# A graph layer on one core: a weight slice loaded ahead of the edge line, transposes behind three products, and a new order for gathers and sums

## The chip, the core and the metric

The kernel runs on one core of a Trainium2 chip. The core has a matrix engine (TensorE, called PE in the profile, with its weight loads as PEld), a vector engine (VectorE, DVE), an activation engine (ScalarE, ACT), a general engine (GpSimd, POOL) and a queue engine for transfers (SyncE, SP). Each engine works through its own list of instructions strictly in order and waits on semaphores for the others. The metric is the device time of one execution in microseconds, as the median of several executions. The kernel before takes 260.74 us as the median of three (260.15, 260.74 and 263.15 us).

## The reference

A layer of a relational graph network on 625 nodes of width 512 and 20,625 edges, sorted by destination, followed by a feed-forward net. Cut to what matters:

```python
h   = relu(layernorm(x))                                  # 625 x 512
msg = sum over r of (h[src] @ W_rel[r] + b_rel[r]) * where(edge_type == r, edge_weight, 0)
agg = segment_sum(msg, dst) / max(segment_sum(edge_weight, dst), 1)
x1  = layernorm(h + h @ W_self + b_self + agg, ln1)
ffn = gelu(x1 @ W_ffn1 + b_ffn1) @ W_ffn2 + b_ffn2        # 512 -> 1024 -> 512
out = x + layernorm(x1 + ffn, ln2)
```

## The kernel before

The nodes lie in five blocks of 128 rows (block 1 has 113). The **first part** makes a table of 20 x 128 rows, the product of every block with each of the four relation weights, scaled and with the bias added. For each of the 20 steps `table_rows` (L391) puts four products into one accumulation bank; one 128x512 product in plain fp32 is two PE instructions in the profile (L403). VectorE scales the result (L416) and SP stores it to the table in memory. During the first relation the transposed form of the next block is made between the products: `between()` turns it with four transposes (L351) into a bank, and ScalarE copies it out (L357) for the next step. The loads at the program's start stand in one list on SP (L262 to L278): halves of x, four slices of the first relation's weight, the line of edges that the first address arithmetic reads, further blocks of x, and so on. SP works through them in that order. In the same part GpSimd scatters 45 columns of edge weights into a memory area of cells (L686), from which the sums of the first and last block are later made as dense products (L1302, L613).

The **second part** handles the blocks in between by gathers. GpSimd issues 99 indirect transfers of 128 table rows each (L1159) and six smaller-purpose ones of the same size (L1216, the first edges of a block that begin in a foreign group). They go into ten buffers called `ms`. Three gathers make one group: ScalarE scales the first row into a PSUM bank called `add` (L1165), VectorE adds the second and the third (L1183), and PE multiplies the sum with a one-hot matrix and accumulates it by destination node. This last product comes in two forms. A **whole** sum is written to SBUF by the third addition (`es`) and multiplied in plain fp32 (L1208). A **parted** sum stays in the bank; ScalarE casts a high part (`eh`, L1169), VectorE subtracts it to get a low part (`el`, L1173), and PE multiplies both in the fp32r format (L1205, L1206). The groups are worked by blocks: single tiles of the outer boundaries first, then block 1, the boundary of 1 and 2, block 2, the boundary of 2 and 3, and block 3 with nine groups and one single tile at the end. When a block's sums are complete VectorE normalises it, PE transposes it (L351), ScalarE copies it (`x1T`, L1363), PE makes the 1024 hidden values in eight pieces (L928), ScalarE applies the gelu to each piece (L932) and PE makes the 512 outputs (L946). The feed-forward nets follow in the block order 0, 4, 1, 2, 3.

The order of everything in the second part on every engine is laid out when the program is built. The class `Plan` walks through time with an estimate for each operation and lets each engine take the operation of best rank among those that are ready; the resulting lists are then fixed. For a gather it assumes a landing `LAND` after its issue, and for the earliest gathers `LATE` more: pairs of a gather number and the addition for gathers below it. Which groups are parted is decided by `parted` from the pair `PARTED` (of the second number of consecutive groups the first number are parted). Idle PE time in the last block's tail is filled with small dummy products (`spin`, L1226).

Of the kernel before, what the change touches and what calls it, by code (L numbers as in the profile page):

```python
# [154 lines left out]
def gnn_layer(ctx, tc, x, edges, edge_line, edge_groups, w_self, w_rel, w_ffn1, w_ffn2, rows_in, bf1_in, out, n_edges):  # L155
# [19 lines left out]
    KD = D // P  # L175
# [52 lines left out]
    def load_x(b0, b1):  # L228
        nc.sync.dma_start(xs[:, b0:b1, :], x[ep.first[b0]:ep.first[b0] + (b1 - b0) * P, :].rearrange("(b p) d -> p b d", p=P))

    def load_wr(r, ks=((0, KD),)):
        wr_sb.setdefault(r, None)
        if wr_sb[r] is None:
            wr_sb[r] = early.tile([P, KD, D], F32, tag="wr", name=f"wr_{r}", bufs=2)
        for k0, k1 in ks:
            nc.sync.dma_start(wr_sb[r][:, k0:k1, :],
                              w_rel[r, :, k0:k1, :])
# [27 lines left out]
    load_wr(0, [(1, 2)])  # L265
    load_x(1, 2)
    load_wr(0, [(2, 3)])
    load_line(0)
    load_wr(0, [(3, 4)])
    load_x(2, 3)  # L270
    load_rows(brel_bc[:, :D], 0, D)
    load_x(3, NB)
# [121 lines left out]
    def table_rows(r, i, between=None):  # L394
        c = r * NB + i
        cuts = (0, 3 * D // 4, D) if c == NC - 1 else (0, D)
        at = [slice(*h) for h in zip(cuts, cuts[1:])]
        p = [buffer("ps") for h in at]
        for p_, h in zip(p, at):
            for k in range(KD):  # L400
                if k == KD // 2 and between:
                    between()
                nc.tensor.matmul(p_[:, :h.stop - h.start], hT[i][:, k, :], wr_sb[r][:, k, h],  # L403
                                 start=(k == 0), stop=(k == KD - 1))
        if c >= NL:
            m = kept[c] = const.tile([P, D], F32, name=f"m_{c}")
        else:
            k = (c + NL) % CH
            if k == 0 or c == 0:
                kept["pair"] = const.tile([P, CH, D], F32, tag="tr", name=f"tr_{c}", bufs=LA)  # L410
            m = kept["pair"][:, k, :]
            if c in held:
                kept[OUTER[0], c] = m
        row0 = r * NP + i * P
        for p_, h in zip(p, at):
            made_row.append(nc.vector.scalar_tensor_tensor(m[:, h], p_[:, :h.stop - h.start], rx[:, i, 1:2],  # L416
                                           brel_bc[:, r * D + h.start:r * D + h.stop], op0=ALU.mult, op1=ALU.add).ins)
            stored.append(nc.sync.dma_start(table[row0:row0 + P, h], m[:, h]).ins)
# [589 lines left out]
    SUM = 3  # L1008
    WARM = 24
    ES = 7  # L1010
    LAND, LATE = 3.6, ((8, 2.0), (40, 1.2))
    HOTS_AT, SELF_AT, ADDS_AT = (15, 16, 17), 15, (16, 17, 18)
    OHS = 3
    OW = 5
# [1 line left out]
    GATHER = 1.26  # L1016
    SLACK = 1.2
    LATER = 0.3
    PARTED = 1, 1
    BEHIND = 5  # L1020
    CELLS = 3.0
    FIRST_PIECE = 4
# [102 lines left out]
    order_of = sorted(of_sum, key=lambda bs: (not set(bs) & set(OUTER), -bs[0] if set(bs) & set(OUTER) else bs))  # L1125
# [37 lines left out]
    def first_row(j, ms, box):  # L1163
        box["sum"] = buffer("add")
        nc.scalar.activation(box["sum"], ms[j], AF.Copy, scale=wgt[:, j:j + 1])  # L1165
# [6 lines left out]
        box["low"] = edge.tile([P, D], F32R, tag="es", name=f"el_{j}", bufs=ES)  # L1172
        nc.vector.tensor_sub(box["low"], box["sum"], box["high"].bitcast(F32))  # L1173

    def parted(k, units):
        return len(units[k]) > 1 and k % PARTED[1] < PARTED[0] and k + 3 < len(units)

    def row_added(j, ms, box, parts):
        k, q = divmod(j - GROUP0, EG)
# [51 lines left out]
    for bs in order_of:  # L1231
        tiles = of_sum[bs]
        units = []
# [13 lines left out]
        for k, unit in enumerate(units):  # L1247
# [15 lines left out]
            for q, (j, g) in enumerate(zip(unit, got)):  # L1263
                alone, whole = len(unit) == 1, q == len(unit) - 1
                if alone:
                    h = g
                elif q == 0:
                    h = row0 = op("ACT", 0.69, lambda j=j, box=box: first_row(j, ms, box), after=[g],
                                  take=["add"], give=[("ms", g)], lag=SLACK, rank=rank)
                else:  # L1270
                    parts = parted(k, units)
                    h = op("DVE", 0.75, lambda j=j, box=box, parts=parts: row_added(j, ms, box, parts), after=[g, h],
                           take=["es"] if whole and not parts else [],
                           give=[("ms", g)] + ([("add", row0)] if whole and not parts else []), lag=LATER, rank=rank)
                    h_last = h
                    if whole and parts:
                        h = op("ACT", 0.65, lambda j=j, box=box: high(j, box), after=[h], take=["es"], rank=rank)
                        h = op("DVE", 0.7, lambda j=j, box=box: low(j, box), after=[h], take=["es"], give=[("add", row0)], lag=0.6, rank=rank, level=0.7)
            end = unit is units[-1]
            parts = parted(k, units)  # L1280
            m = op("PE", 0.47 if parts else 0.87,
                   lambda bs=bs, k=k, q=k - k0, end=end, ohs=ohs, box=box, j=unit[0]: edge_sum(bs, k, q, end, ohs, box, j),
                   after=[h, hots_op, m], take=["acc"] if k == 0 else [],
# [290 lines left out]
```

## Time and profile before

| quantity | value |
|---|---|
| median of the timed executions | 260.74 us |
| the profiled execution | 262.26 us |
| its span from the first to the last instruction | 260.5 us |
| PE busy | 246.4 us, 95% |
| VectorE busy | 200.5 us, 77% |
| GpSimd busy | 172.0 us, 66% |
| ScalarE busy | 74.8 us, 29% |

A row of the timeline gives the start in us, the duration in us (of several merged instructions if it ends in x4, x16 and so on), the engine, the line, the operation and its tiles; a bracket holds the idle time of the engine just before it and what ended that. A row of the chain gives start, duration, engine, tile and line. A row of a table by stretches gives the stretch, its length, and for PE, PEld, DVE, ACT and POOL the busy time and the number of instructions, then the granted PE clock, the share of the transfer engines and GB/s.

### The profile page before, as it was taken

Reading aid. Unit: us, or ns where it says so; the run is one execution under the profiler, and the core shown is the slowest. Engines: PE = TensorE matmul, PEld = TensorE weight load, DVE = VectorE, ACT = ScalarE, POOL = GpSimd, SP = SyncE. Lnnn points to the kernel's source line nnn. Section 1 sums busy time; section 2 is a strip of 40 time slices with the busy share of each in tenths; the row PEclk is TensorE's granted clock in tenths of the full one; section 3 lists DMA queues with packets and bytes.
Section 4 is the critical chain, followed back from the end, with each engine's and each line's share of the span. In section 5 each row is a group of like instructions: output and inputs, shape, how many; then the busy total and the mean of one; then the engine's idle time right before and its main releaser. Section 6 shows DMA issues by size and latency. Waiting matters only on the chain. (4 is left out here: it accounts for less than half of the span.)

```text
span 260.5 us, 3515 instructions
## 1 busy us (share of the span) xinstructions
PE 246.4 (95%) x1051; PEld 141.4 (54%) x1051; DVE 200.5 (77%) x503; ACT 74.8 (29%) x224; POOL 172.0 (66%) x230
## 2 busy tenths in 40 slices
PE   8899999999999969999959999989999998899996
PEld 6444444445445625443424444864685964675964
DVE  2896999997979964839879399997798985973614
ACT  3017300000031573623121142641223632310420
POOL 4478889887888577777778777777777777100000
PEclk9999999999999999999999999999999999799999
DMA  5999999972272599799997977777776677330101
GB/s 191 361 402 416 379 382 360 321 285 81 73 253 85 199 363 328 227 346 299 367 325 219 374 232 201 218 191 208 213 212 205 199 204 213 111 110 6 44 0 44
DMA packets 24055, 60.20 MB, mean 231 GB/s; under 512 B 4401, under 2 KB 8753, under 8 KB 22882
## 3 DMA queue, kind: packets, MB, share of 16 engines
q0 software_dynamic: 9936, 27.58, 35.0%
q1 hardware_dynamic: 13808, 30.94, 32.1%
q10 hardware_dynamic: 290, 1.44, 1.6%
q8 instruction: 9, 0.15, 0.2%
q14 instruction: 12, 0.10, 0.1%
HBM read 50.77 MB, written 9.17 MB: 230 GB/s over the span
## 5 line engine op out<-in xcount | busy, mean ns | idle before, releaser
L1159 POOL DMA_INDIRECT ms<-table,row_i x99 | 97.2, 982 | 30.8 <-issue 13.4
L403 PE MATMUL ps<-wr,hT 128*128 128x512 f32 (+2 forms) x168 | 71.2, 576 | 0.0
L686 POOL DMA_INDIRECT cells<-weight,cell x45 | 48.6, 1080 | 9.0 <-issue 6.4
L403 PEld LDWEIGHTS ps<-wr,hT 128*128 128x128 f32 x168 | 30.6, 190 | 33.8 <-issue 29.9
L1183 DVE SCALAR_TENSOR_TENSOR add<-ms,wgt_g,add 128x512 f32<-128x512 f32 x48 | 35.7, 748 | 16.8 <-DMA ms<-table,row_i 14.9
L928 PEld LDWEIGHTS ps<-x1T,w_sb 128*128 128x128 f32 x320 | 39.1, 197 | 5.2 <-issue 3.2
L928 PE MATMUL ps<-x1T,w_sb 128*128 128x128 f32 (+1 forms) x320 | 39.7, 281 | 0.9 <-ACT gT L932 0.9
L1165 ACT ACTIVATE add<-ms,ed 128x512 f32<-128x512 f32 x30 | 20.7, 692 | 66.5 <-DMA ms<-table,row_i 47.3
L946 PE MATMUL ps<-w_sb,gT 128*128 128x512 f32 (+3 forms) x96 | 36.2, 522 | 0.0
L1302 PE MATMUL acc<-tr,sums_w 128*128 128x512 f32 x60 | 27.7, 595 | 0.0
L599 ACT ACTIVATE ohw<-os,w 128x128 fp32r<-128x128 f32 x36 | 11.4, 389 | 56.3 <-DVE os L581 55.3
L946 PEld LDWEIGHTS ps<-w_sb,gT 128*128 128x128 f32 (+1 forms) x96 | 16.6, 188 | 14.4 <-issue 11.8
L932 ACT ACTIVATE gT<-ps,bf 128x128 f32<-128x128 f32 (+1 forms) x40 | 13.3, 362 | 19.6 <-PE ps L928 14.9
L441 PE MATMUL ps<-ws_sb,hT 128*128 128x512 f32 x40 | 18.3, 592 | 0.0
L1302 PEld LDWEIGHTS acc<-tr,sums_w 128*128 128x128 f32 x60 | 11.0, 190 | 12.3 <-issue 11.2
L1208 PE MATMUL acc<-es,oh 128*128 128x512 f32 x24 | 12.9, 626 | 3.2 <-DVE es L1183 3.2
L416 DVE SCALAR_TENSOR_TENSOR tr<-ps,rx,brel_bc 128x512 f32<-128x512 f32 x15 | 11.2, 744 | 3.3 <-POOL idle L689 2.1
L1173 DVE TENSOR_TENSOR el<-add,eh 128x512 fp32r<-128x512 f32 x18 | 12.3, 681 | 0.9 <-ACT eh L1169 0.8
L1169 ACT CAST eh<-add 128x512 fp32r<-128x512 f32 x18 | 10.5, 581 | 8.2 <-DVE add L1183 8.2
L956 DVE TENSOR_TENSOR ow<-ps,z 128x512 f32<-128x512 f32 (+3 forms) x6 | 3.6, 599 | 11.4 <-PE ps L946 11.3
L441 PEld LDWEIGHTS ps<-ws_sb,hT 128*128 128x128 f32 x40 | 7.6, 190 | 8.7 <-issue 8.6
L1205 PE MATMUL acc<-eh,oh 128*128 128x512 f32 x18 | 11.7, 651 | 0.0
(215 smaller groups left out, 302.5 us busy)
## 6 DMA issues: line engine op xcount, KB each, us to landing
tr<-table SPq DMA_DIRECT2D x11, 512.0 KB, 6.3
w_sb<-in_L_gnn_W_ffn_dram SPq DMA_DIRECT2D x2, 2048.0 KB, 9.5
table<-tr SPq DMA_DIRECT2D x15, 256.0 KB, 6.3
wr<-in_L_gnn_W_rel_dram SPq DMA_DIRECT2D x3, 1024.0 KB, 8.8
cells<-zeros SPq DMA_DIRECT2D x2, 1280.0 KB, 12.5
ms<-table,row_i POOLq DMA_INDIRECT x99, 3.8
rows<-in_rows_dram SPq DMA_DIRECT2D x1, 1536.0 KB, 13.0
sums_w<-cells ACTq DMA_DIRECT2D x1, 1280.0 KB, 5.9
```

The source lines that it names most:

```text
L403: nc.tensor.matmul(p_[:, :h.stop - h.start], hT[i][:, k, :], wr_sb[r][:, k, h], start=(k == 0), stop=(k == KD - 1))
L441: nc.tensor.matmul(p[0], hT[i][:, k, :], ws_sb[:, k, :], start=(k == 0), stop=(k == KD - 1))
L686: s = nc.gpsimd.indirect_dma_start(out=cells[i][:, :], out_offset=bass.IndirectOffsetOnAxis(ap=cell[i][:, k:k + 1], axis=0), in_=weight[i] ...
L928: nc.tensor.matmul(pu[:, :nn], w1_sb[:, k, f * P:(f + 1) * P], x1T_b()[:, k, :nn], start=(k == 0), stop=(k == KD - 1))
L932: nc.scalar.activation(box["gT"][:, f, :nn], pus[f][:, :nn], AF.Gelu, bias=bf1[:, f:f + 1])
L946: nc.tensor.matmul(po[h][:n, :w], box["gT"][:, f, at], w2_sb[:, f, c], start=(f == 0), stop=(f == KF - 1))
L1159: nc.gpsimd.indirect_dma_start(out=ms[j], out_offset=None, in_=table[:, :], in_offset=bass.IndirectOffsetOnAxis(ap=row_i[:, j:j + 1], axis=0))
L1165: nc.scalar.activation(box["sum"], ms[j], AF.Copy, scale=wgt[:, j:j + 1])
L1173: nc.vector.tensor_sub(box["low"], box["sum"], box["high"].bitcast(F32))
L1183: nc.vector.scalar_tensor_tensor(to, ms[j], wgt_g[:, k, q - 1:q], box["sum"], op0=ALU.mult, op1=ALU.add)
L1208: nc.tensor.matmul(acc[bs], ohs[0][:, q, :].bitcast(F32), box["sum"] if "sum" in box else ms[j], start=(k == 0), stop=last)
L1302: nc.tensor.matmul(acc[b,], sums_w[b][:, c, :], kept[(b, c) if (b, c) in kept else c], start=first, stop=last)
```

## The change

It has four parts. The fourth slice of the first weight is issued on SP ahead of the line of edges instead of behind it. In the first relation the next block's transposes are put in behind three of a step's four products instead of two. The plan's addition to the landing of early gathers becomes 3.5 us below gather 8, 2.5 us below gather 56 and 0.5 us below gather 120, which is all the rest. And two of three groups are parted instead of all; the last three groups of a block, whole until now, may be parted too except in the last block.

```diff
@@ loads at the start
     load_wr(0, [(2, 3)])
+    load_wr(0, [(3, 4)])
     load_line(0)
-    load_wr(0, [(3, 4)])
     load_x(2, 3)
@@ table_rows
-                if k == KD // 2 and between:
+                if k == KD - 1 and between:
                     between()
@@ constants
-    LAND, LATE = 3.6, ((8, 2.0), (40, 1.2))
+    LAND, LATE = 3.6, ((8, 3.5), (56, 2.5), (120, 0.5))
-    PARTED = 1, 1
+    PARTED = 2, 3
@@ parted
-    def parted(k, units):
-        return len(units[k]) > 1 and k % PARTED[1] < PARTED[0] and k + 3 < len(units)
+    def parted(bs, k, units):
+        return len(units[k]) > 1 and k % PARTED[1] < PARTED[0] and (k + 3 < len(units) or bs != order_of[-1])
```

The count of parted sums goes from 18 to 21, that of whole ones from 12 to 9; within the last block it goes from seven to five.

On PE, at the start of the program, the products of step 0 and 1 (`L403`, bank `ps_81` and `ps_79`) and the transposes between them (`L351`):

```order
-L403 MATMUL ps_81<-wr_103,hT_146 128x512 x2
+L403 MATMUL ps_81<-wr_103,hT_146 128x512 x3
 L351 MATMUL ps_78<-ident,z 128x128 x4
-L403 MATMUL ps_81<-wr_103,hT_146 128x512 x2
-L403 MATMUL ps_79<-wr_103,hT_147 128x512 x2
+L403 MATMUL ps_81<-wr_103,hT_146 128x512
+L403 MATMUL ps_79<-wr_103,hT_147 128x512 x3
```

One product of the step is left behind the transposes, where there were two.

On PE, where the last block's groups 6, 7 and 8 (of 0 to 8) and its single tile stand beside block 2's feed-forward net (`x1T_1752` and `gT_1855`), before the change, from group 6's two parts to the single tile `ms_951` and on to the last block's transposes (`ident,ow_953`):

```order
L1205 MATMUL acc_1_1701<-eh_1849,oh_1726 128x512
L1206 MATMUL acc_1_1701<-el_1852,oh_1726 128x512
L1208 MATMUL acc_1_1701<-es_1860,oh_1726 128x512
L928 MATMUL ps_78<-x1T_1752,w_sb 128x128 x4
L928 MATMUL ps_81<-x1T_1752,w_sb 128x128 x4
L928 MATMUL ps_80<-x1T_1752,w_sb 128x128 x4
L1208 MATMUL acc_1_1701<-es_1891,oh_1844 128x512
L1208 MATMUL acc_1_1701<-ms_951,oh_1874 128x512
L928 MATMUL ps_79<-x1T_1752,w_sb 128x128 x4
L928 MATMUL ps_78<-x1T_1752,w_sb 128x128 x4
L928 MATMUL ps_81<-x1T_1752,w_sb 128x128 x4
L946 MATMUL ps_80<-w_sb,gT_1855 128x512 x4
```

The same place of the changed kernel, where block 2's net reads `x1T_1832` and `gT_1850` and the single tile is `ms_947`; the row ahead is the last of block 2's eight L928 rows:

```order
L928 MATMUL ps_81<-x1T_1832,w_sb 128x128 x4
L1205 MATMUL acc_1_1730<-eh_1877,oh_1779 128x512
L1206 MATMUL acc_1_1730<-el_1897,oh_1779 128x512
L1208 MATMUL acc_1_1730<-es_1890,oh_1779 128x512
L946 MATMUL ps_79<-w_sb,gT_1850 128x512 x2
L1208 MATMUL acc_1_1730<-es_1929,oh_1883 128x512
L1208 MATMUL acc_1_1730<-ms_947,oh_1911 128x512
L946 MATMUL ps_79<-w_sb,gT_1850 128x512 x6
L351 MATMUL ps_78<-ident,ow_957 128x128 x2
L351 MATMUL ps_80<-ident,ow_957 128x128 x2
```

All of block 2's hidden products now stand ahead of group 6, and six output products are left behind the single tile, where there were five hidden pieces and eight output products (three of the former and four of the latter ahead of the transposes).

On ScalarE, changed kernel, at the start of block 2's gelus (`gT_1850`): `add_82<-ms_949` and `add_83<-ms_950` are the first rows of the last block's groups 6 and 7.

```order
L1363 COPY x1T_1832<-ps_80 128x512
L1165 ACTIVATE add_82<-ms_949,ed 128x512
L1165 ACTIVATE add_83<-ms_950,ed 128x512
L932 ACTIVATE gT_1850<-ps_79,bf_92 128x128
L932 ACTIVATE gT_1850<-ps_78,bf_92 128x128
L1169 CAST eh_1877<-add_82 128x512
L932 ACTIVATE gT_1850<-ps_80,bf_92 128x128
```

Before the change the row directly ahead of this block's first gelu was the first row of group 8; now it is the first row of group 7, and group 6's cast has moved in between the gelus.

More of the change, by code (lines that the diff above doesn't have):

```diff
@@ L1270, in gnn_layer @@
                 else:
-                    parts = parted(k, units)
+                    parts = parted(bs, k, units)
                     h = op("DVE", 0.75, lambda j=j, box=box, parts=parts: row_added(j, ms, box, parts), after=[g, h],
@@ L1279, in gnn_layer @@
             end = unit is units[-1]
-            parts = parted(k, units)
+            parts = parted(bs, k, units)
             m = op("PE", 0.47 if parts else 0.87,
```

## The prediction

> **What bounds the kernel now.** I read the page first, then a table by stretches, then the chain of waits, and last the rows of single engines at the places where PE stands still. In the stretches the third number is PE's busy time, the granted PE clock stands behind POOL's count.
>
> ```profile
> span 260.5 us, 3515 instructions
> 88.00:100.00 12.00, 9.91 (x34) 5.17 (x33) 7.33 (x32) 8.26 (x25) 9.17 (x10) 1.00 0.97 359
> 100.00:133.50 33.50, 33.04 (x100) 15.36 (x99) 24.40 (x46) 11.92 (x20) 25.58 (x27) 1.00 0.92 309
> 133.50:137.00 3.50, 0.47 (x2) 0.27 (x2) 2.48 (x4) 0.69 (x1) 2.59 (x4) 1.00 0.90 314
> 137.00:176.00 39.00, 37.39 (x145) 21.78 (x145) 33.95 (x70) 13.56 (x26) 29.86 (x31) 1.00 0.77 239
> 176.00:220.00 44.00, 43.77 (x215) 28.84 (x214) 36.06 (x80) 15.54 (x35) 33.64 (x35) 1.00 0.72 207
> 220.00:223.00 3.00, 1.10 (x6) 0.48 (x4) 2.13 (x4) 0.75 (x2) 2.05 (x3) 1.00 0.75 202
> 223.00:240.00 17.00, 17.00 (x75) 11.42 (x76) 10.96 (x28) 3.12 (x10) 1.01 (x1) 0.90 0.20 70
> ```
>
> PE is idle for 2.1 us in the first stretch, 0.5 in the second, 3.0 in the third, 1.6 in the fourth, 0.2 in the fifth and 1.9 in the sixth, and in the last it runs at a lower clock. From 176 to 220 it has no gap to speak of, so an earlier gap is not made up there: PE is behind, and its backlog sets the end. The other resource is GpSimd's list of gathers.
>
> ```profile
> 88.09 1.10 POOL L1159 DMA_INDIRECT ms<-table,row_i  x1 [0.94 <-DVE od L591]
> 221.72 0.94 POOL L1159 DMA_INDIRECT ms<-table,row_i  x1 [0.30 <-DVE add L1183]
> DMA to landing us min/median/max: 3.6/3.8/6.6
> ```
>
> The first gather is issued at 88.09, the last at 221.72, 105 in all: 104 steps of 1.28 us, each an issue of 0.95 and the 0.30 that the bracket shows. It hardly waits for a buffer. The last landing is therefore near 221.72 + 3.8 = 225.5, whatever PE does. The chain that ended last shows how the two meet (start, duration, engine, tile, line):
>
> ```profile
> 215.48 5.30 DMA ms<-table,row_i
> ...
> 222.93 1.52 PE acc L1208 x2
> 224.45 3.93 PE ps L928 x24
> 228.38 1.72 PE acc L1208 x4
> 230.09 2.68 PE ps L928 x24
> 232.77 3.44 PE ps L946 x8
> ...
> 236.65 3.44 PE ps L946 x8
> 240.08 7.14 PE ps L928 x64
> ```
>
> One gather of the last block's group 7 took 5.30 us instead of 3.8; behind its addition VectorE had the low part of group 6, and PE waited for that. The same chain shows the price: two sums of four instructions take 1.72, so a whole sum is 0.86, but at 222.93 one took 1.52; 24 instructions of L928 take 2.68, but at 224.45 they took 3.93. The last block's sum is complete at 230.09, and its own feed-forward net begins at 240.08. Everything behind 240.08 stays as it is, so the question is where this mark moves.
>
> **The change part by part.** *Parted sums.* A pair of parts costs PE the distance from 163.09 to 163.56:
>
> ```profile
> 163.09 0.39 PE L1205 MATMUL acc<-eh,oh 128*128 128x512 f32 x1
> 163.33 0.39 PE L1206 MATMUL acc<-el,oh 128*128 128x512 f32 x1
> 163.56 1.95 PE L928 MATMUL ps<-x1T,w_sb 128*128 128x128 f32 x16
> ```
>
> That is 0.47 against 0.86, 0.39 saved for each of three more parted sums: 1.2 us of PE, all of it ahead of group 6. They cost ScalarE a cast and VectorE a subtraction each:
>
> ```profile
> L1169 ACT CAST eh<-add 128x512 fp32r<-128x512 f32 x18 | 10.5, 581 | 8.2 <-DVE add L1183 8.2
> L1173 DVE TENSOR_TENSOR el<-add,eh 128x512 fp32r<-128x512 f32 x18 | 12.3, 681 | 0.9 <-ACT eh L1169 0.8
> ```
>
> 1.7 and 2.0 us in all. Between 176 and 220 VectorE has 44 - 36.1 = 7.9 us free and ScalarE 28.5, so I take them as hidden; if that cover fails, a sum comes 1.3 us later and PE waits that long. In the last block two groups fewer are parted, which takes 2 x 0.39 = 0.8 from PE's gain there (it is in the 1.2) and 2 x 1.3 us from the latency of its sums.
>
> *Later gathers in the plan.* This adds no instruction; it puts more ready work ahead of products that wait. Three places can be read from the rows and the new order.
>
> ```profile
> 94.57 1.10 PE L1208 MATMUL acc<-ms,oh 128*128 128x512 f32 x2 [1.82 <-issue]
> 134.51 0.75 DVE L429 SCALAR_TENSOR_TENSOR z<-ms,x_on,rows 64x512 f32<-64x512 f32 x1 [1.89 <-DMA ms<-table,x_row]
> 136.73 1.12 PE L1208 MATMUL acc<-es,oh 128*128 128x512 f32 x2 [3.03 <-DVE es L1183]
> ```
>
> At 94.57 PE had stood 1.82 us for the first gather, which takes over 6 us there (88.09 to 94.57). Now two more pairs of bank products and one dense product of 0.86 stand ahead, about 1.8 in all: this gap goes (0 to 1.8; I take 1.8). At 136.73 PE had stood 3.03 us, because VectorE stood 1.89 for a foreign first row and the awaited sum was behind it. The new order has two more self products and three more dense ones ahead, 5 x 0.86 = 4.3 us, but the two sums awaited now are parted and their low parts stand further back in VectorE's list, behind five more operations of 0.7: I count 0.6 less idle (0 to 3.0). Together the gaps close by 2.4; a gap of the same kind appears at the next pair of first rows, where the order puts both ahead of two low parts, so I keep 2.0 of at most 6.7 (the idle from 88 to 176), and as the other end -2.0, the gaps growing as much.
>
> At the end of the program, block 2's up-projection begins at 218.35 now:
>
> ```profile
> 218.35 1.95 PE L928 MATMUL ps<-x1T,w_sb 128*128 128x128 f32 x16
> 217.99 0.69 ACT L1165 ACTIVATE add<-ms,ed 128x512 f32<-128x512 f32 x1 [2.48 <-DMA ms<-table,row_i]
> L932 ACT ACTIVATE gT<-ps,bf 128x128 f32<-128x128 f32 (+1 forms) x40 | 13.3, 362 | 19.6 <-PE ps L928 14.9
> ```
>
> From PE alone it would begin at 218.35 - 1.2 - 2.0 = 215.2. It has four banks, so the fifth of its eight pieces (7.14 / 8 = 0.89 each) waits for the first gelu, and ScalarE's list now has the first row of group 7 ahead of that, which lands at 217.99 and takes 0.69; with a gelu of 0.36 the fifth piece starts at 219.05 at the earliest and the eighth ends at 222.6. If PE is late instead (gaps unchanged), it begins at 217.2 and ends at 224.3. Then come, in the new order, a parted sum, a whole sum, two output products, a whole sum and the single tile: 0.47 + 5 x 0.86 = 4.8. The last block's sum is complete at **227.4 to 229.1** instead of 230.09. The gathers allow it: the last lands at 225.5, the one before it 1.25 earlier.
>
> Behind it PE has six output products, 5.2 us, and then the transposes. What the last block's normalisation takes is read here:
>
> ```profile
> 231.48 0.74 DVE L429 SCALAR_TENSOR_TENSOR z<-acc,rdeg,z 128x512 f32<-128x512 f32 x1
> 236.46 0.65 ACT L1363 COPY x1T<-ps 128x256 f32<-128x256 f32 x2 [2.12 <-PE ps L351]
> ```
>
> From 231.48 to 236.46 + 0.65 are 5.6 us; with the end of the sum and the first weight I take 6.0. The dummy products put behind the transposes lie inside it. So the mark moves from 240.08 to **233.4 to 235.1**. Of today's ten microseconds between the last sum and the mark four go, because the backlog is now worked off ahead of the sum; that is no saving of PE work, and the balance is this: 1.2 of parted sums, 1.9 of idle time and 1.9 of slow clock (0.66 at 222.93 and 1.25 at 224.45) give 5.0, the earlier gaps up to 1.7 more before the gelu limits.
>
> *The clock.* After the gap at 220 the rows show this:
>
> ```profile
> 224.00:225.00 1.00, 1.00 (x5) 0.76 (x4) 1.00 (x4) 0.00 (x0) 0.00 (x0) 0.50 0.46 184
> ```
>
> A gap of 1.9 us was followed by a clock of 0.50, and the gap of 3.03 us at 133.7 by none (1.00 in both stretches around it). A new gap may thus cost about 1.9 more or nothing, so I put 0.8 on the mark for it and for what I don't see: **234.2**. [...]
>
> *The front.* It decides when the gathers start, for the table must be stored first.
>
> ```profile
> 86.83 0.31 POOL L701 MEMSET idle<- 128x2 bf16 x1 [1.54 <-DMA table<-m]
> 2.62 0.43 SPq L236 DMA_DIRECT2D wr<-in_L_gnn_W_rel_dram  x1
> L403 PEld LDWEIGHTS ps<-wr,hT 128*128 128x128 f32 x168 | 30.6, 190 | 33.8 <-issue 29.9
> 8.75 0.66 PE L351 MATMUL ps<-ident,z 128*128 128x128 f32 x4 [0.91 <-DVE rx L368]
> 9.24 3.60 PE L403 MATMUL ps<-wr,hT 128*128 128x512 f32 x8
> 9.44 0.59 ACT L357 COPY hT<-ps 128x512 f32<-128x512 f32 x1 [3.41 <-PE ps L351]
> wr<-in_L_gnn_W_rel_dram SPq DMA_DIRECT2D x4, 256.0 KB, 5.3
> ```
>
> PE stands 0.91 us ahead of the transposes; the third product fills it if its weight slice is there. That is issued at 2.62, lands 5.3 later at 7.9, so the gap goes and the transposes begin 0.2 later: a gain of about 0.5 to 0.9. Against it the copy to the next step ends at 10.03, 0.79 behind the start of the products at 9.24; with a weight load of 0.19 the one product left, 0.86, falls 0.1 to 0.2 short at each of four steps, 0.4 to 0.8. The line of edges lands one slice later, up to 0.6 us for VectorE's first address work, with GpSimd's scatters behind it; GpSimd then waits 1.54 us for the table's last store, so this is covered. I take 0 for the front, with -0.9 to +0.6.
>
> **The sum.** 234.2 - 240.08 = -5.9 us. The profiled execution took 262.26 us (span 260.5 and 1.8 around it) and would take 256.4. It lies 1.5 above the median of the runs, 260.74, inside their 260.15 to 263.15; on the median the sum is **254.8 us**.
>
> **The rivals.** *The gaps only move.* For it: a fixed order is only as good as its landings, which run here from 3.6 to 6.6 us; the plan's later landing is an average, and the gap at 220 came from one slow transfer, which some other product may meet. Against it: at the end eight pieces of ready work now stand ahead of group 6. Then only the parted sums stay, 260.74 - 1.2 = 259.5, and with a gelu that comes late up to 261. It also covers the case that the new table does nothing it says.
>
> *Gathers begin to wait.* The ten buffers come round after 10 x 1.25 = 12.5 us, and a landing takes 3.8 to 6.6 of that, so a row may be read 6 to 8 us after it is there. A plan that believes landings to be 2.5 to 3.5 us later reads later, and VectorE's list carries the foreign first rows, which stop all additions behind them (1.89 at 134.51). From the point at which a row is read more than 8 us late GpSimd stands, and every microsecond goes to the last landing one to one; a whole group late is 3 x 1.25 = 3.75, at the three pairs of first rows 11.3, and the time 254.8 + 11.3 = 266. To be slower by over 1% it needs 8.5 of these. Against it: all of GpSimd's brackets show 0.30 today, and the reads I followed in the new order come 2 to 4 us before the buffer is wanted.
>
> **How the numbers follow.** About 1% (2.6 us) is what a measurement here can tell from no change: under 258.1 is faster, over 263.3 slower. The forecast, 252.6 to 257, has 0.62. The gaps that only move have 0.27, of them 0.08 end under 258.1, 0.17 within 1%, 0.02 above. Waiting gathers have 0.11, of them 0.01 within 1% and 0.10 above. That makes 0.70 faster, 0.18 same, 0.12 slower. The lower end is the mark at 233.4 (254.1), less the front's 0.9 and the 0.6 by which the fastest run lies below the median: 252.6. The upper end takes in the moved gaps, 261.5, and leaves out the waiting gathers.
>
> **What would show it.** Right: no gap of PE over 1 us between 215 and the last block's net, no clock of 0.50 there, that net's first instruction near 234, group 6 directly behind eight pieces of L928, the last gather still issued at 221 to 222, no 1.82 at 94. Wrong: brackets of POOL over 0.30 at L1159 (the second rival); a PE gap of 2 us or more between 130 and 215 with a clock below 1.00 behind it, and the mark near 239 (the first); PE brackets at L403 of over 0.3 at each of the first steps (the front). Most likely to fail is the count of gaps before 215, since I followed each list only at the places named.

## The result, and the profile after

The changed kernel takes **259.18 us** (median of 20 executions, 257.27 to 263.1). Beside it the kernel before took 261.82 (20 executions, 259.64 to 263.45); the first three of them, whose median was the 260.74 above, lay low. The ratio, taken without the few executions that were slow as a whole, is **0.9918, 95% interval 0.9897 to 0.994**: a gain of 0.8%, 2.1 us by this ratio and 2.6 by the two medians, where 5.9 were forecast. The profiled execution took 258.68 us, 3.6 less than the one before.

The page and the table by stretches of the changed kernel, columns as in the prediction; the stretches are bounded by its own gaps:

```profile
span 256.9 us, 3522 instructions
88.00:100.00 12.00, 10.79 (x37) 5.50 (x36) 7.55 (x31) 8.25 (x24) 9.26 (x10) 1.00 0.98 362
100.00:136.50 36.50, 36.00 (x106) 16.30 (x104) 26.13 (x49) 11.92 (x20) 27.67 (x30) 1.00 0.91 310
136.50:139.00 2.50, 0.65 (x3) 0.29 (x2) 2.50 (x5) 0.89 (x2) 1.89 (x3) 1.00 1.01 360
139.00:176.00 37.00, 37.00 (x145) 21.87 (x145) 32.82 (x68) 14.93 (x28) 28.17 (x30) 1.00 0.78 241
176.00:217.50 41.50, 40.14 (x222) 28.32 (x221) 36.77 (x74) 14.87 (x33) 31.94 (x32) 1.00 0.72 205
217.50:220.00 2.50, 0.67 (x6) 0.48 (x5) 0.81 (x2) 1.34 (x4) 1.89 (x2) 1.00 0.75 236
220.00:234.40 14.40, 14.40 (x67) 8.95 (x66) 12.51 (x38) 3.61 (x10) 2.92 (x3) 1.00 0.33 101
```

From 88 to 176 PE is idle for 3.6 us instead of 7.2, from 176 to the last net's start for 3.2 instead of 2.1, and its clock is 1.00 in every stretch. The chain of waits at the end, then the row at which PE waits there:

```profile
219.69 3.84 PE ps L928 x32
...
223.99 0.86 PE acc L1208 x2
224.85 1.72 PE ps L946 x4
226.56 1.72 PE acc L1208 x4
228.28 5.15 PE ps L946 x12
...
234.41 7.15 PE ps L928 x64
```
```profile
219.69 3.84 PE L928 MATMUL ps<-x1T,w_sb 128*128 128x128 f32 x32 [1.83 <-ACT gT L932]
```

The last block's sum is complete at 228.28 and its net begins at **234.41**, which is 5.67 us earlier than 240.08. So in this execution the mark, the start of the last block's net, moved as forecast, although PE stands 1.83 us for the first gelu where no gap was expected. The missing two microseconds lie behind the mark: from 240.08 to the end of the span were 20.4 us, from 234.41 they are 22.5. PE, VectorE and ScalarE repeat their rows there to within 0.1 us; the difference is in the last two stores. First the kernel before, its issue on SP, GB/s in 40 slices of 0.15 us from 254.5 to 260.5, and the stores' size and landing; then the changed kernel, from 250.9 to 256.9:

```profile
257.05 0.81 SPq L997 DMA_DIRECT2D out_dram<-ow  x2
GB/s 0 0 0 0 0 0 0 0 0 0 0 0 0 55 0 0 0 0 0 0 0 0 102 358 358 282 304 287 57 0 109 0 0 0 0 0 0 0 0 0
out_dram<-ow SPq DMA_DIRECT2D x1, 160.0 KB, 1.8
out_dram<-ow SPq DMA_DIRECT2D x1, 96.0 KB, 1.7
```
```profile
251.39 0.81 SPq L997 DMA_DIRECT2D out_dram<-ow  x2
GB/s 0 0 0 0 0 0 0 0 51 324 324 282 263 302 256 0 0 0 0 0 0 9 9 9 9 26 19 26 5 0 0 0 0 0 0 0 0 0 0 0
q8 instruction: 1, 0.02, 1.0%
out_dram<-ow SPq DMA_DIRECT2D x1, 160.0 KB, 4.0
out_dram<-ow SPq DMA_DIRECT2D x1, 96.0 KB, 3.8
```

The stores are issued 5.66 us earlier, but land in 4.0 and 3.8 us instead of 1.8 and 1.7. Their traffic stops at 253.1 as it should and then trickles from 254.1 to 255.2. The same view of the changed kernel from 253.2 to 255.4 counts what trickles:

```profile
DMA packets 18, 0.02 MB, mean 7 GB/s; under 512 B 2, under 2 KB 18, under 8 KB 18
```

Eighteen of 288 packets are a sixteenth. The views count 16 transfer engines, so this would be one engine's share if the packets are spread evenly; which engine took a packet is not in the list. In the trace's list of packets the first of them starts at 254.12. Just ahead of it stands one packet of 16,384 bytes on the queue q8, whose kind the view gives as instruction, from 253.14 to 254.14; it is called PE's code fetch here. It begins 1.04 us behind the end of the last dummy product of PE (252.10), where PE's list goes on with the branch of `L1442`; that it is PE's own is read from this and from the runs below, in which it moves with PE's dummy products. In the kernel before this packet begins at 259.04 (the 109 in its row), behind the last packet of the stores. That the branch called for this packet is not shown: the trace has PE's first instruction behind the branch (a DRAIN at 252.29) before the packet begins.

One thing the list leaves open. The other fifteen sixteenths of the store begin from 252.22 on, and the late eighteen had not begun by 253.14 either, when the fetch is recorded to start. What held them in this 0.9 us is not in the list of packets; in the repeat of this kernel the same stretch is 0.28 us.

### The profile page after: what moved, and what is told of

It is laid out like the page before. It is cut to its first block, busy times and chain, and to the rows that moved or that the text cites. A ratio compares the mean times of both kernels' runs of the same rounds, so it can differ in the third digit from the quotient of the medians.

```text
span 256.9 us, 3522 instructions
## 1 busy us (share of the span) xinstructions
PE 242.9 (95%) x1051; PEld 138.9 (54%) x1051; DVE 201.5 (78%) x505; ACT 77.0 (30%) x227; POOL 173.4 (67%) x230
## 4 chain that ended last, share of the span: by engine, by line
PE 55%; DMA 21%; DVE 15%; issue 4%; POOL 2%; ACT 1%; SPq 0%; DVEq 0%; POOLq 0%; ACTq 0%
PE ps L403 26%; DMA ms<-table,row_i 15%; PE acc L1302 7%; PE ps L946 5%; PE ps L928 4%; DMA ms<-table,x_row 4%; DVE add L1183 4%; PE acc L1208 4%; DVE z L429 3%; DVE el L1173 2%; POOL ms L1159 2%; DMA wr<-in_L_gnn_W_rel_dram 2%; PE ps L613 2%; PE spin L1226 2%; PE ps L441 1%
## 5 line engine op out<-in xcount | busy, mean ns | idle before, releaser
L403 PE MATMUL ps<-wr,hT 128*128 128x512 f32 (+2 forms) x168 | 71.6, 578 | 0.4 <-DMA wr<-in_L_gnn_W_rel_dram 0.4
L686 POOL DMA_INDIRECT cells<-weight,cell x45 | 50.4, 1119 | 8.0 <-issue 6.8
L403 PEld LDWEIGHTS ps<-wr,hT 128*128 128x128 f32 x168 | 30.2, 190 | 35.0 <-issue 29.0
L1183 DVE SCALAR_TENSOR_TENSOR add<-ms,wgt_g,add 128x512 f32<-128x512 f32 x51 | 38.0, 748 | 6.2 <-DMA ms<-table,row_i 3.2
L928 PEld LDWEIGHTS ps<-x1T,w_sb 128*128 128x128 f32 x320 | 37.1, 192 | 4.7 <-issue 2.4
L928 PE MATMUL ps<-x1T,w_sb 128*128 128x128 f32 (+1 forms) x320 | 37.6, 275 | 1.8 <-ACT gT L932 1.8
L1302 PE MATMUL acc<-tr,sums_w 128*128 128x512 f32 x60 | 27.9, 596 | 0.0
L1169 ACT CAST eh<-add 128x512 fp32r<-128x512 f32 x21 | 12.3, 584 | 17.3 <-DVE add L1183 16.3
L1302 PEld LDWEIGHTS acc<-tr,sums_w 128*128 128x128 f32 x60 | 11.0, 190 | 11.5 <-issue 10.5
L1173 DVE TENSOR_TENSOR el<-add,eh 128x512 fp32r<-128x512 f32 x21 | 14.1, 680 | 3.1 <-ACT eh L1169 3.1
L1205 PE MATMUL acc<-eh,oh 128*128 128x512 f32 x21 | 13.3, 632 | 0.0
L1206 PE MATMUL acc<-el,oh 128*128 128x512 f32 x21 | 9.1, 434 | 3.4 <-DVE el L1173 3.4
```

The source lines that it names most:

```text
L686: s = nc.gpsimd.indirect_dma_start(out=cells[i][:, :], out_offset=bass.IndirectOffsetOnAxis(ap=cell[i][:, k:k + 1], axis=0), in_=weight[i] ...
L928: nc.tensor.matmul(pu[:, :nn], w1_sb[:, k, f * P:(f + 1) * P], x1T_b()[:, k, :nn], start=(k == 0), stop=(k == KD - 1))
L1183: nc.vector.scalar_tensor_tensor(to, ms[j], wgt_g[:, k, q - 1:q], box["sum"], op0=ALU.mult, op1=ALU.add)
L1205: nc.tensor.matmul(acc[bs], ohs[0][:, q, :], box["high"], start=(k == 0), stop=False)
L1302: nc.tensor.matmul(acc[b,], sums_w[b][:, c, :], kept[(b, c) if (b, c) in kept else c], start=first, stop=last)
```

## The experiments

**Is the late store chance, and does the fetch cause it?** Both kernels were run once more, and the dummy products (`spin`, `L1287`) of both were varied, since the packet on q8 follows the last of them, 0.51 us behind it in the kernel before and 1.04 in the changed one.

The kernel before, unchanged.

> The kernel before once more, unchanged, for a second profiled execution and for the span and clock of every run. Theory: the stall of 1.9 us at 220 and the clock of 0.50 at 224 belong to the program's order, so both stand there again, the last block's own net starts at 240.1 (within 0.5), and the last two stores land in 1.7 to 1.8 us, because PE's last code fetch comes behind their packets. Rival: the dip of the clock is an accident of the one execution shown; then the net starts near 238.5 and the gain of the change is 1.5 us smaller than it looked. Span 260.5 by the first, 259 by the second.

Measured: span 260.5 us, median 262.61, stores in 1.8 and 1.7 us, and the net again at 239.92 by the timeline (which gives 239.92 for the first execution's 240.08 too). But the clock's dip was not at 224: it stood at 137.6 to 141.0, and the clock from 215 on was 1.00. So the place of the dip is accidental. The last block's sum was complete at 228.7 here, 1.4 us earlier than in the first execution, and the net started no earlier, so the mark doesn't hang on the dip at 224 alone. What does hold it then is read from VectorE and PE of this execution:

```profile
227.67 1.02 PE L1208 MATMUL acc<-ms,oh 128*128 128x512 f32 x2
229.70 0.75 DVE L966 SCALAR_TENSOR_TENSOR ow<-ow,mv_y,rows 128x512 f32<-128x512 f32 x1 [1.81 <-DMA out_dram<-ow]
231.68 0.74 DVE L429 SCALAR_TENSOR_TENSOR z<-acc,rdeg,z 128x512 f32<-128x512 f32 x1
235.84 0.80 PE L351 MATMUL ps<-ident,ow 128*128 128x128 f32 x4 [1.04 <-DVE ow L892]
```

The sum is complete at 228.7, but VectorE takes it up (L429) only at 231.68: an operation on another block's output (L966) stands ahead of it and waits 1.81 us for an output buffer that is still being stored. PE then waits 1.04 for the transposes' input. The first execution has the same wait (1.82 at 229.50), hidden behind PE's slow clock.

The changed kernel, unchanged.

> The changed kernel once more, unchanged, beside the runs of the kernel before on the same chip as the others of this call. Theory: the order sets the mark only to about 1 us, since the landings of the gathers vary: the net starts between 234.2 and 236, the stores again take 3.8 to 4.0 us, the ratio is 0.990 to 0.993. Rival: the late packets of the store were an accident; then they land in 1.8 us and the ratio is 0.983.

Measured: ratio 0.9899 (0.9858 to 0.994); net at 233.55; stores in 3.3 and 3.1 us. The fetch ran from 251.81 to 252.90 and 18 packets began at 252.89. The late share came again, as the first theory has it, but mark and stores both lie below the bounds that it gave (234.2 and 3.8).

The changed kernel with short, then with long dummy groups; then the kernel before with short ones as control.

```diff
-                    op("PE", 0.55, lambda: spin(5), after=[m], take=["one"], give=["one"], rank=rank, level=9)
+                    op("PE", 0.55, lambda: spin(1), after=[m], take=["one"], give=["one"], rank=rank, level=9)
```

> The changed kernel with one product in each spin instead of five (spins are PE work whose output nobody reads). In the profile of the changed kernel the net started 5.67 us earlier and the last store was issued 5.66 us earlier, yet the span fell by 3.6 us only: the last two stores took 4.0 and 3.8 us to land instead of 1.8 and 1.7, and 18 of their 288 packets came 2 us behind the others, right behind a code fetch of 16 KB that began at 253.14, 1.04 us behind PE's last spin. Theory (the code fetch that follows the spins stands in front of one DMA engine's share of the store): the spins end 2.9 us earlier and the fetch with them, ahead of the store; the stores land in 1.7 to 1.8 us; the spin ahead of the net is 0.5 us shorter too; span 256.9 - 2.0 - 0.4 = 254.5 us, ratio to the kernel before 0.982 to 0.985. Rival (the store is late for another reason, or only in that one execution): the stores land as in the changed kernel, span 256.5, ratio 0.990 to 0.992.

Measured: ratio **0.980** (0.9748 to 0.9853), median 257.54. The fetch ran from 252.10 to 253.12, the stores were issued at 252.73 and their packets ran from 253.56 to 254.49 without a late share; in the view from 250.4 to 256.4:

```profile
GB/s 0 0 0 0 0 0 0 0 0 0 0 164 0 0 0 0 0 0 0 0 0 273 341 358 268 328 174 60 0 0 0 0 0 0 0 0 0 0 0 0
out_dram<-ow SPq DMA_DIRECT2D x1, 96.0 KB, 1.9
```

Span 256.4 instead of 254.5 in this execution, since its net came late, at 235.49; the ratio, over all executions, lies a little below the 0.982 to 0.985 of the theory, with both inside its interval.

With `spin(9)`:

> The changed kernel with nine products in each spin. Theory (code fetch): the spins at the end last 2.9 us longer, end near 255.4 and the fetch comes behind the packets of the stores, which land in 1.7 to 1.8 us as before; the spin ahead of the net costs 0.5 us more; span 256.9 + 0.5 - 2.0 = 255.4 us, or up to 256.8 if the program's end waits for PE; ratio 0.985 to 0.990. Rival (another reason): the stores still take 3.8 to 4.0 us, span 257.4, ratio 0.994.

Measured: ratio 0.9846 (0.9803 to 0.989), stores 2.7 us. PE's fetch began at 255.89, behind all packets, as foretold; the 2.7 was a miss. One last packet of the store began at 255.06, behind an instruction packet of 8 KB on another queue (254.72 to 255.07), and 0.3 us behind all others; why the store then counts as landed only 1.0 us after that is not shown. With more dummy work the kernel was faster than the changed one (0.9846 against 0.9918, the intervals just apart; against the other two measurements of the changed order, e4 and e11, they overlap).

The control:

> The kernel before with one product in each spin instead of five, the control to the changed kernel with short spins. In the kernel before all six spins stand at the very end and PE's last code fetch, at 259.04, begins 0.2 us behind the last packet of the stores. Theory (the fetch that follows the spins hurts only where it meets the store): the spins end 3.4 us earlier, the fetch starts near 255.6, ahead of the store's packets at 257.9, the stores still land in 1.7 to 2.0 us, and nothing is gained: span 260.0 to 260.7, ratio 0.997 to 1.002. Rival (the spins cost time at the end of any kernel): span 258.5, ratio 0.990 to 0.993.

Measured: ratio 1.0008 (0.9977 to 1.0039), stores 2.2 us. The control is not quite free of the fetch: it ran from 255.81 to 257.10, over the first packets of the store (256.93), and the second store's packets came about 0.5 us late as a whole, which a late sixteenth does not explain. Still, short dummy groups gain nothing where no collision stood before, so the gain of the changed kernel with them is the collision's, as far as the intervals can tell (0.1 us of it is the shorter dummy group ahead of the net).

The other way round: a collision made in the kernel before, by taking work away.

```diff
-                    op("PE", 0.55, lambda: spin(5), after=[m], take=["one"], give=["one"], rank=rank, level=9)
+                    op("PE", 0.55, lambda: spin(4), after=[m], take=["one"], give=["one"], rank=rank, level=9)
```

> The kernel before with four products in each spin instead of five: its last spin then ends near 257.7 instead of 258.5, and the code fetch that follows it should begin at 258.1 to 258.4, amid the packets of the last stores (257.9 to 258.8). Theory (a code fetch on one transfer engine holds up that engine's share of the store): less work, and yet later: 18 of the 288 packets come 1 to 2 us behind the others, the two stores land in 3 to 4 us, span 261.5 to 262.5, ratio 1.004 to 1.008. Rival (the late packets have nothing to do with the fetch): stores in 1.7 to 2.2 us, ratio 0.998 to 1.001.

Measured: ratio **1.0046** (1.0016 to 1.0077), slower with less work, by little. The collision was half of what was expected: the fetch ran from 256.93 to 257.89, nine packets instead of 18, a sixteenth of the second store's 144, began at 257.88, only that store was late, and the span of this execution, 260.2, was no longer than before (GB/s from 254.2 to 260.2):

```profile
GB/s 0 0 0 0 55 0 0 0 0 0 0 0 0 0 171 375 350 249 420 231 21 0 0 0 5 10 10 10 5 0 0 0 0 0 0 0 0 0 0 0
out_dram<-ow SPq DMA_DIRECT2D x1, 160.0 KB, 1.9
out_dram<-ow SPq DMA_DIRECT2D x1, 96.0 KB, 3.0
```

That settles what costs the time at the end: the fetch's place was moved in both directions, and the store's late share came and went with it. In four profiled executions (the changed kernel twice, with its front undone, and this one) the first late packet starts within 0.02 us of the end of PE's fetch; with the long groups (e3) the one late packet follows an 8 KB packet of another queue in the same way, 255.06 against 255.07. The traces record packets, not what holds an engine; the 0.9 us above stays open.

**The front.** Its two edits taken back in the changed kernel:

```diff
-    load_wr(0, [(3, 4)])
     load_line(0)
+    load_wr(0, [(3, 4)])
@@ table_rows
-                if k == KD - 1 and between:
+                if k == KD // 2 and between:
```

> The changed kernel without its two edits at the front: the line of edges is loaded ahead of the last piece of the first weights again, and the next block's transposes stand in the middle of a row's last products again. Forecast's term: the front is worth nothing (gain of 0.9 to loss of 0.6 us), the start of the sums stays at 83.6 to 83.9 and the ratio at 0.990 to 0.994. Rival: the front hides the gain; in the changed kernel the second to fifth transposes come 0.3 to 0.7 us later than before, so undoing it makes the kernel 0.3 to 0.7 us faster, ratio 0.989. Other rival: the front brings part of the gain (the sums start 0.24 us earlier with it), ratio 0.993 to 0.995 without.

Measured: ratio 0.9909 (0.9871 to 0.9947), net at 234.23, the first sum product (L1302) at 83.64 instead of 83.57; stores 4.0 and 3.8, the collision again. The front is worth nothing that these intervals, about 1 us to each side, can show.

**Which table brings the gain?** Each alone on the kernel before, with short dummy groups; the control is 1.0008.

```diff
-    LAND, LATE = 3.6, ((8, 2.0), (40, 1.2))
+    LAND, LATE = 3.6, ((8, 3.5), (56, 2.5), (120, 0.5))
```

> The kernel before with nothing of the change but the table of later landings (no parted sums exchanged, front as before), and with short spins, so that the store meets no code fetch and the place of the last net can be read. Forecast's terms: without the parted sums (1.2 us) the net starts near 235.5 to 236.5, ratio 0.985. Rival, from the new order: two products more than with the whole change stand between the last transposes and the net (1.72 us), and half of the last up-projection still stands behind group 6, so the net starts at 237.5 to 239, ratio 0.990 to 0.995: the gain needs both tables.

Measured: ratio 0.9958 (0.9923 to 0.9993), net at 238.14, clock 0.50 from 139.6 to 143.0.

```diff
-    PARTED = 1, 1
+    PARTED = 2, 3
@@ parted
-        return len(units[k]) > 1 and k % PARTED[1] < PARTED[0] and k + 3 < len(units)
+        return len(units[k]) > 1 and k % PARTED[1] < PARTED[0] and (k + 3 < len(units) or bs != order_of[-1])
```

> The kernel before with nothing of the change but the parting of two of three groups, and with short spins. Forecast's term: 1.2 us, the net at 238.9, ratio 0.995. Rival, from the new order: here too two products stand between the transposes and the net instead of four, which is worth 1.7 us if the sum is not later, so the net starts at 237.5 to 238.4, ratio 0.989 to 0.992. Other rival: the gaps grow as much as the parts save, ratio 1.000.

Measured: ratio 0.9895 (0.9838 to 0.9953), net at 236.24, earlier than any theory had it. For both, the rival read from the order came closer than the forecast's terms. In both, VectorE still waits 1.82 us for the store ahead of the last sum, and the stores meet the fetch as in the control (2.4 us). Together the two tables, with the front, bring 2.0% (e2) against the 1.6% that 0.5 and 1.1, measured against the control, add up to; the intervals are wider than the difference.

**What VectorE's wait costs the kernel before.** The plan is told that an output buffer comes back 3.5 us behind its store; PE's order stays the same.

```diff
-                                [("ow", made["y0"]), ("ow", made["a"])] if name == "stored" else [], rank=None)
+                                [("ow", made["y0"]), ("ow", made["a"])] if name == "stored" else [], lag=3.5 if name == "stored" else 0.08, rank=None)
```

> The kernel before with short spins, and the plan told that an output buffer comes back 3.5 us behind its store instead of at once. By that VectorE's list has the last block's sum ahead of the product that waits for a store's buffer; PE's list is the same. In three executions of the kernel before that product waits 1.82 us for a store, and the last block's sum stands behind it on VectorE, 1.4 to 3.0 us late. Theory A (that wait holds the net up where PE has no backlog): the gap of 1.05 us ahead of the last transposes goes and the net starts 1.0 us earlier, at 238.0 with a dip of the clock before 215 or none; ratio 0.995 to 0.997. Theory B (PE's backlog, as forecast): the net starts where it did, 239 to 240, ratio 1.000.

Measured: ratio 0.9968 (0.9928 to 1.0008). The execution profiled had no dip ahead of the end, and its rows are

```profile
227.33 0.75 DVE L429 SCALAR_TENSOR_TENSOR z<-acc,rdeg,z 128x512 f32<-128x512 f32 x1
232.73 0.60 PE L351 MATMUL ps<-ident,ow 128*128 128x128 f32 x4
236.60 7.31 PE L928 MATMUL ps<-x1T,w_sb 128*128 128x128 f32 x64
```

The sum is complete at 226.8 (its last row starts at 225.75 and lasts 1.02) and is taken up 0.6 later, instead of 3.0 in the control; the gap of 1.05 ahead of the transposes is gone. The net is 2.4 earlier than in the control (238.96), of which 1.05 is that gap, 0.9 the sum's earlier end and the rest lies in the rows around the transposes. Theory A by the rows, though the 0.9 cannot be told from what the control's dip of the clock at 138.4 cost it; the time alone, 0.4% less than the control with intervals that overlap, would not have decided it.

**What PE's wait at 219.69 costs the changed kernel.** In the plan alone the first gather of group 7 lands 2.5 us later (short dummy groups):

```diff
-    ... lag=LAND + next((late for most, late in LATE if n < most), 0.0), ...
+    ... lag=LAND + next((late for most, late in LATE if n < most), 0.0) + (2.5 if n == 92 else 0.0), ...
```

> The changed kernel with short spins, and in the plan alone the first gather of the last block's group 7 is taken to land 2.5 us later; by that ScalarE has the first two gelus of block 2 ahead of that group's first row, and nothing else ahead of them moves. In the changed kernel PE stood 1.83 to 2.17 us at this place, waiting for the first gelu. Theory A (that wait is paid in full): the wait goes, the sum is complete 1.7 us earlier and the net starts 1.7 us earlier relative to the last gather than with short spins alone; ratio 0.973 to 0.975. Theory B (the gathers' end binds there too: the last one is issued at 221.5 to 222.5, lands 3.8 later, and an addition and two sums follow): the sum is complete 0 to 0.5 us earlier, ratio 0.978 to 0.981.

The row of PE's wait in this run:

```profile
220.88 2.05 PE L928 MATMUL ps<-x1T,w_sb 128*128 128x128 f32 x16 [0.94 <-ACT gT L932]
```

Measured: ratio 0.9818 (0.9769 to 0.9868), so in time no different from short dummy groups alone. By the rows the wait fell from 2.17 to 0.94, now ahead of the seventh piece, and the net's start, counted from the last gather's issue, from 13.0 (235.49 - 222.47) to 12.2 us (233.89 - 221.72). Two thirds of what went of the wait came through to the mark. The edit did more than was expected of it, though: in PE's list two more output products moved ahead of the last block's sum, and one more dummy group ahead of the net. So the sum was complete later by the same count (7.7 us instead of 7.2), against both theories, and from the last hidden piece to the net PE had 11.2 us of work instead of 10.8, without a gap in either. That is the third that did not come through: PE's list, not the gathers' end, binds there.

All edits that cost nothing, together (front undone, short dummy groups, the gather's later landing):

> The changed kernel with the front undone, short spins, and the first two gelus of block 2 ahead of the last block's group 7 in the plan: all edits that did not cost anything. Theory: the front is worth nothing and the gelus 0 to 0.5 us, so it is as fast as the short spins alone, ratio 0.978 to 0.982. Rival: the gains add up, ratio 0.972 to 0.976.

Measured: ratio 0.9813 (0.9772 to 0.9855), median 256.44, the net at 232.67 with a wait of 0.25 left, span 253.5, stores 1.8 and 1.9. The gains don't add up beyond what the intervals can show. This and the short dummy groups alone beat both kernels.

## Why the prediction was wrong, step by step

*Everything behind 240.08 stays as it is.* **This step failed.** It was stated without a row, and it carried 20.4 us of the time; in the changed kernel the same stretch takes 22.5. The new order has one of the six dummy groups ahead of the net, so PE's last dummy product ends 0.7 us behind the store's issue (252.10 and 251.39) instead of 1.5 (258.53 and 257.05), and the code fetch behind it moved towards the store: it begins 1.1 to 1.75 us behind the store's issue in three executions of the changed order's end, and 1.87 and 1.99 in two of the kernel before, where the packets are through by then. Its price is 2.1 us in the profiled execution and 2.0 on the mean of three with the changed order's end (stores 4.0, 3.3 and 4.0 against 1.8).

*The mark at 234.2 (233.4 to 235.1).* Right in the profiled execution, 234.41, and so is the sum's end, 228.28 (227.4 to 229.1). The 6.0 us from there to the net are right by luck, as they were read as the time of the normalisation: VectorE had the transposes' input ready at 232.2 (L892), and what filled the 6.1 us was PE's own list, 5.15 of output products, 0.44 of transposes and 0.54 of a dummy group. As a typical figure the mark was 1.3 us too good: by the timeline's rows the net started at 239.92, 239.92, 238.96 and 238.38 in four executions of the kernel before with nothing changed ahead of the net, and at 234.25, 233.55, 234.23, 235.49 and 235.84 in five of the changed order (the last two have the dummy group ahead of the net 0.1 us shorter and 0.4 longer). The means are 239.3 and 234.7: the shift is **-4.6**. Half of the 1.3 is the first execution of the kernel before, whose net started later than the mean of its order, the other half the changed order itself. With 2.0 for the store the shift gives -2.6, which is what the medians show (259.18 - 261.82); the ratio has 2.1.

*The balance of 1.2, 1.9 and 1.9.* The parted sums are right as a direction (e7), but the account is wrong in what held the mark. The second execution of the kernel before had a full clock at 224, and its net started at the same time, for VectorE took the last sum up 3.0 us late. The row with the wait for the store, 229.50 in the execution forecast from, was not read. In the changed order nothing stands ahead of that sum: L429 starts at 228.32, 0.04 behind it.

*No gap over 1 us from 215 on.* Wrong: 1.83, and 1.35 to 2.17 in the other executions of that order. The prediction had itself worked out that the fifth piece waits for the first gelu until 219.05 at least; it began its up-projection at 215.2, where that leaves a wait of 0.3, while PE came to it at 214.12. So the gap moved from the sum to the gelu, half of the first rival, and cost up to 1.4 us of the mark (e12 against e2, by the same count from the last gather: 11.6 against 13.0, PE's list in e12 being that of e8).

*The earlier gaps.* The idle time from 88 to 176 fell by 3.6 us, from 7.2 to 3.6, where 2.0 were kept (the prediction's 6.7 leaves out the 0.5 of its second stretch). But it fell elsewhere than was worked out: the gap at 94.57, which was to go whole, is still 1.21 at 95.14; the 3.03 at 136.73, of which 0.6 was to go, is 1.85 at 138.71; and the 1.6 between 137 and 176, for which nothing was counted, went altogether. The direction is right, the size is partly luck. *The front at 0:* right. *The clock:* no dip in the changed kernel, where the sum had put 0.8 aside for one and for what was not seen. *Waiting gathers:* wrong as a rival, the brackets of POOL behind its first gather stayed at 0.30, and the last gather was issued at 221.45, inside the 221 to 222 forecast.

*From the profiled execution to the median.* It was scaled down by 1.5 us on three runs; with 20, the profiled 262.26 was 0.4 above the median. On its own time the forecast was 256.4. The range, 252.6 to 261.5, held the time, and "faster by over 1%", the likeliest case, did not come: 0.8%.

## What to carry to other kernels

A step that says "behind here nothing changes" needs rows like any other: list what else falls into that stretch (stores, code fetches, the end of other engines), and ask whether a shift moves it onto something. When PE looks like the bound, look for what stands ahead of the awaited operation in the other engines' lists too, above all for waits on a store's buffer. And before a gain of two per cent is forecast from one execution, its places (dips, gaps) should be seen in a second one.

## What the runs showed of the hardware

**The code fetch and the store.** PE's last packet of 16 KB took 0.96 to 1.69 us, and in four executions 18 of the stores' 288 packets, or nine, began within 0.02 us of its end. In the changed kernel the last of the 18 ended at 255.17, and the two stores landed in 4.0 and 3.8 us instead of 1.8 and 1.7. The fetch began 0.02 to 1.41 us behind PE's last dummy product in every run, so here its place could be set by a few products nobody reads: with 4 instead of 5 per group the kernel before lost 0.5%, with 1 instead of 5 the changed one gained 1.2%.

**Where the clock dipped in these executions.** The trace of the first execution records its dip with 3.413 us, from 223.53 to 226.95. Each dip ahead of the end lasted 3.41 us and began a whole multiple of 3.413 us behind the moment at which the clock of that execution first was full (5.08 in the first execution: 223.53 is 64 multiples later; 137.59 in the second is 39 behind its 4.47). Divided into stretches of this length from that moment on, the executions look like this around their gaps, each stretch with the one behind it, first the kernel before, then it with short dummy groups, then the later landings alone, then the changed kernel with long groups:

```profile
134.79:138.20 3.41, 1.47 (x4) 0.75 (x5) 3.38 (x6) 0.69 (x1) 2.80 (x3) 1.00 0.78 245
138.20:141.60 3.40, 3.40 (x10) 1.49 (x9) 3.35 (x7) 0.69 (x1) 2.49 (x4) 1.00 0.61 181
220.12:223.53 3.41, 1.51 (x6) 0.65 (x5) 2.55 (x5) 1.23 (x3) 1.93 (x3) 1.00 0.74 219
223.53:226.94 3.41, 3.41 (x15) 2.90 (x14) 3.34 (x10) 0.37 (x1) 0.00 (x0) 0.50 0.28 82
```
```profile
134.94:138.35 3.41, 0.71 (x2) 0.47 (x3) 2.92 (x5) 0.58 (x1) 2.80 (x3) 1.00 0.90 309
138.35:141.77 3.42, 3.42 (x5) 1.36 (x5) 3.38 (x6) 0.80 (x2) 2.81 (x3) 0.50 0.49 146
```
```profile
136.18:139.59 3.41, 0.98 (x3) 0.15 (x1) 3.40 (x6) 0.69 (x1) 2.80 (x3) 1.00 0.85 266
139.59:143.00 3.41, 3.34 (x4) 1.51 (x5) 2.24 (x6) 0.69 (x1) 2.50 (x4) 0.50 1.00 340
```
```profile
135.37:138.78 3.41, 1.79 (x5) 0.57 (x3) 3.33 (x6) 0.06 (x1) 2.65 (x3) 1.00 1.02 383
138.78:142.20 3.42, 2.52 (x7) 1.35 (x8) 3.42 (x8) 1.91 (x3) 2.51 (x4) 1.00 0.99 369
```

With PE busy 0.71 or 0.98 us of 3.41 a dip followed; 1.51 had one and 1.47 none; 1.79 none. Divided in the same way, all fourteen profiled executions agree ahead of the last dummy products: each of the five stretches with up to 1.28 us busy was followed by a dip, none with 1.66 or more was, and of the three in between 1.47 and 1.49 were not and 1.51 was. That is a count over these executions; what makes the clock dip is in no trace, and the ends of products are modelled in the profile. The last two kernels have gaps of the same length (2.50 and 2.51 us), one almost wholly inside a stretch and the other spread over two. What a dip cost where PE was busy: ten instructions of L1302 that took 4.46 us at a clock of 1.00 took 6.15 in the kernel before, run again, 1.7 more. The five profiled executions of the changed order had no dip ahead of the end, all four of the order before had one or two (with VectorE's list changed, in e10, there was none). Stretches that were a third busy (1.06 and 1.28 us of 3.41) were followed by a dip too. What would be left of the changed kernel's gain without the dips of the kernel before was not tried.
